# A graph layer on one core: how the node features x come into SBUF and are transposed

## The chip, the cores and the metric

The kernel runs on one core of a Trainium2 chip. What counts is the time of one execution on the device in microseconds (us). A core has five engines with instruction streams of their own: PE (matrix multiplications and transposes), DVE (elementwise work), ACT (elementwise work, copies), POOL (elementwise work, indirect DMAs) and SP (which here only issues DMAs). The transfers that SP, ACT and POOL issue share 16 DMA engines.

## The reference

Inputs are x (6250 nodes by 128 values, float32), and 100,000 edges, src and dst, sorted by dst. For each edge a small network works on the features of its two ends, the results are averaged over the edges that end in a node, and a second network and a layer norm follow:

```python
msg_in = concatenate([x[src], x[dst]], axis=-1)
h = relu(msg_in @ Wm1 + bm1)
h = relu(h @ Wm2 + bm2)
messages = h @ Wm3 + bm3
agg = segment_sum(messages, dst) / clip(count, 1)
upd = relu(concatenate([x, agg]) @ Wn1 + bn1) @ Wn2 + bn2
out = layernorm(x + (x + upd))
```

## The kernel before, in words

The first layer is split: x[src] @ (upper half of Wm1) and x[dst] @ (lower half) are worked out once per node, not once per edge. So there are three stages.

**Preparation**, up to about 85 us. x is loaded into `x_sb` (L172 to L180): tile t holds rows 128 t to 128 t + 127, one row on each partition, so a DMA of n tiles puts n separate rows of 512 bytes on each partition. The DMAs take 2, 2, 4, 8, 8, 8, 8 and 8 tiles, and one more takes the last 106 rows. Four tiles make a block, and there are 13 blocks (12 full ones and the rest). `turn` (L256 to L263) transposes a block's tiles on PE into one bank `pt` (L261), and ACT copies the bank to `xT` (L263), which holds x with nodes along the free axis. `a_table` (L234) multiplies two tiles of `xT` with one half of Wm1 (`products`, L230), ACT copies the products to a buffer of the pool `brow` (L239), and SP writes them to the table `atab` in HBM (L240). `b_table` (L242) does the same with the other half of Wm1 and splits the products into three bf16 terms, with ACT (L247), DVE (L248, L253) and POOL or ACT (L250, L252), before SP writes them to `btab` (L254). `brow` has six buffers, which both tables share; a buffer is free again when its write has landed. `x_part` (L304 to L315) works out x's part of the second network and puts it over `xT` and `x_sb`, whose first contents have then been used.

Beside that, `dst` and `src` are loaded (`load_rows`, L129) through ACT's and POOL's queues, DVE works out the window of nodes of each group of edges (L188 to L214, L268), and `starts` and `columns` (L272 to L302) spread it over the partitions. `dpad`, a copy of dst in HBM, is written by SP (L533).

The order of PE's instructions is written by hand (the loop at L329 to L344): transposes of block i + 1, then the products of block i for atab, then those of block i - 3 for btab. Up to the end of this stage the other engines' orders, SP's queue among them, come from a planner, which places instructions by estimated costs when the program is built. Each engine carries out its instructions in the order given, and waits on semaphores for what others produce.

**The edge loop**, to about 1131 us: 196 groups of up to 512 edges. POOL gathers rows of atab (L406), SP loads a window of btab (L412), and PE does the layers (L443, L449, L463) and the sums over nodes (L472, L483).

**The node stage**, to the end: blocks of 512 nodes, with a load of the nodes' reciprocal counts `rc` spread over all partitions (L662), the second network and the layer norm.

Of the kernel before, what the change touches and what calls it, by code (L numbers as in the profile page):

```python
# [19 lines left out]
P = 128  # L20
EPS = 1e-5
NONE = 16384
WN = 32
# [4 lines left out]
def kernel(  # L28
# [36 lines left out]
    nc = tc.nc  # L65
    N, D = x.shape
# [3 lines left out]
    GT = 4  # L70
# [4 lines left out]
    LT = -(-LAST // P)  # L75
    NT = -(-N // P)
    NTF = N // P
# [2 lines left out]
    R = NG // 2  # L80
    assert D == P and HC == 2 and NG == NGF + 1 and NG == 2 * R and R <= P
    assert E % 16 == 0 and (N - 1) + N // 16 * WB + WB < NONE
    assert LT == 2 and N < NONE and GT * WN == P

    assert N - 1 + WB + 1 <= NPAD and 3 * WB + 1 == NQ

# [10 lines left out]
    x_sb = const.tile([P, NT, D], F32, name="x_sb")  # L97
    xT = const.tile([P, NT * P], F32, name="xT")
# [30 lines left out]
    def load_rows(eng, t, edges):  # L129

        row = 2 * GE
        full = E // row // 16 * 16
        eng.dma_start(t[:full, :], edges[: full * row].rearrange("(r e) -> r e", e=row))
        for r in range(full, R):
            n = min(row, E - r * row)
            eng.dma_start(t[r:r + 1, :n], edges[r * row:r * row + n].rearrange("(r e) -> r e", r=1))
# [14 lines left out]
    with tc.tile_pool(name="prep", bufs=1) as prep, tc.tile_pool(  # L151
# [9 lines left out]
        with tc.high_priority():  # L161
            nc.scalar.dma_start(w1, wm1.rearrange("(k p) h -> p k h", p=P))
            load_rows(nc.scalar, dst_i, dst)
            load_rows(nc.gpsimd, src_i, src)
            with nc.allow_non_contiguous_dma(reason="a bias, one value a partition"):
                nc.gpsimd.dma_start(b1, bm1.rearrange("(c p) -> p c", p=P))
                nc.gpsimd.dma_start(b2, bm2.rearrange("(c p) -> p c", p=P))
                nc.gpsimd.dma_start(b3, bm3.rearrange("(c p) -> p c", p=P))
                nc.gpsimd.dma_start(bu1, bn1.rearrange("(c p) -> p c", p=P))
            nc.gpsimd.dma_start(nb2[:, 0, :], bm2.rearrange("(o h) -> o h", o=1).to_broadcast([P, H]))  # L170
            t = 0
            for n in (2, 2, 4, 8, 8, 8, 8, 8):  # L172
                n = min(n, NTF - t)
                nc.sync.dma_start(
                    x_sb[:, t:t + n, :],
                    x[t * P:(t + n) * P, :].rearrange("(t p) d -> p t d", p=P),
                )
                t += n
            assert t == NTF
            nc.sync.dma_start(x_sb[:N - NTF * P, NTF, :], x[NTF * P:, :])  # L180
# [75 lines left out]
        def turn(t0):  # L256
            m = min(4, NT - t0)
            pt = pp.tile([P, 4, P], F32, name="pt", tag="pp")
            for i in range(m):
                n = min(P, N - (t0 + i) * P)  # L260
                nc.tensor.transpose(pt[:, i, :n], x_sb[:n, t0 + i, :], ident[:n, :n])  # L261
            w = min(m * P, N - t0 * P)
            nc.scalar.copy(xT[:, t0 * P:t0 * P + w], pt.rearrange("p i n -> p (i n)")[:, :w])  # L263

# [60 lines left out]
        assert sorted(X_BESIDE + X_BEHIND + X_FIRST + X_END) == list(range(BLOCKS))  # L327

        turn(0)  # L329
        for i in range(BLOCKS + BEHIND):  # L330
            if i + 1 < BLOCKS:
                turn(4 * i + 4)
            if i < BLOCKS:
                for t0 in range(4 * i, min(4 * i + 4, NT), 2):
                    a_table(t0)
            if i == INDICES:
                starts()
            if i - INDICES in (1, 2):
                columns(i - INDICES - 1)
            if i >= BEHIND:  # L340
                for t0 in range(4 * (i - BEHIND), min(4 * (i - BEHIND) + 4, NT), 2):
                    b_table(t0)
            if BLOCKS - 1 <= i < BLOCKS - 1 + len(X_BESIDE):
                whole(x_part(X_BESIDE[i - BLOCKS + 1], bank_pb, (nc.scalar, nc.scalar)))  # L344
# [44 lines left out]
    with edge, tc.tile_pool(name="wk", bufs=2) as wk, tc.tile_pool(  # L389
# [136 lines left out]
        for i in range(NG + ahead + 1):  # L526
# [48 lines left out]
            m = g - 1  # L575
# [183 lines left out]
```

## Time and profile before

| what | value |
|---|---|
| median of 3 runs | 1212.57 us (1211.47 to 1213.6) |
| the profiled execution's own time | 1212.32 us |
| its span in the profile | 1210.5 us |
| PE busy | 1180.8 us (98%) |
| DVE, ACT, POOL busy | 669.9, 449.5, 805.9 us |
| first issue of x on SP, end of the last one | 0.77 us, 15.34 us |
| first write to atab issued | 18.79 us |
| first load from btab issued | 83.26 us |

How to read the profile. Times count from the start of the span. In lists of groups a line has: source line, engine, operation, what is written and read, partitions x elements and type, count, then busy us and the mean ns of one, then idle time ahead of them and what ended it. PEld is PE's weight load, which runs beside its multiplications. In the timeline a line has start, length, engine, source line, operation, count, and in brackets the idle time before it and what ended that. A busy PE is not PE at its peak, since the ends of its instructions are modelled. The DMA share is the mean busy share of the 16 DMA engines; it goes over 1 where packets overlap. Queue q1 is SP's, q10 ACT's and q0 POOL's.

### The profile page before, as it was taken

To read this page: it belongs to the slowest core of one execution; us is meant where nothing else is said; L and a number is where in the kernel's file an instruction comes from. 1 tells how busy PE (TensorE), PEld (TensorE's weight loads), DVE (VectorE), ACT (ScalarE), POOL (GpSimd) and SP (SyncE) were. 2 spreads that over 40 slices of the span, in tenths; PEclk is the share of its full clock that TensorE was granted. 3 is DMA by queue.
4 is the path that set the end of the run, shared out by engine and by line. 5 is a ranking of instruction groups with operands and counts; after the bars stand their busy time and mean duration, and the time that the engine had idled before them with its cause. 6 is when DMAs were issued, how large, how long until landed. Compare 5 with 4: busy or idle time off the path is not lost. (4 is left out here: it accounts for less than half of the span.)

```text
span 1210.5 us, 32797 instructions
## 1 busy us (share of the span) xinstructions
PE 1180.8 (98%) x11196; PEld 896.3 (74%) x11197; DVE 669.9 (55%) x2080; ACT 449.5 (37%) x1163; POOL 805.9 (67%) x859
## 2 busy tenths in 40 slices
PE   6989999999999999999999999999999999999996
PEld 5747777777777777777777777777777777777565
DVE  5764555545555555555555555555555555555586
ACT  4563333333333333333333333333333333333256
POOL 8267777777777777777777777777777777773220
PEclk9999999999999999999999999999999999999998
DMA  9886766666555555555555555555555555552333
GB/s 270 289 268 162 190 188 182 190 188 175 151 147 151 154 153 152 149 155 149 147 151 153 153 152 151 152 152 146 152 153 152 153 151 150 147 148 60 99 108 105
DMA packets 178152, 193.66 MB, mean 160 GB/s; under 512 B 30844, under 2 KB 151374, under 8 KB 177968
## 3 DMA queue, kind: packets, MB, share of 16 engines
q0 software_dynamic: 37984, 103.35, 31.0%
q1 hardware_dynamic: 111436, 61.93, 18.0%
q10 hardware_dynamic: 28564, 26.27, 7.9%
q8 instruction: 90, 1.47, 0.5%
q14 instruction: 78, 0.64, 0.2%
HBM read 168.92 MB, written 22.88 MB: 158 GB/s over the span
## 5 line engine op out<-in xcount | busy, mean ns | idle before, releaser
L406 POOL DMA_INDIRECT ag<-atab,srcT x784 | 753.2, 961 | 283.4 <-issue 184.3
L463 PE MATMUL ph<-w,h 128*128 128x256 f32 x3128 | 727.5, 386 | 0.9 <-ACT x_sb L312 0.9
L463 PEld LDWEIGHTS ph<-w,h 128*128 128x128 f32 x3128 | 578.3, 190 | 151.9 <-DVE acc L488 67.8
L454 ACT ACTIVATE h<-ph,b 128x256 f32<-128x256 f32 x782 | 306.3, 475 | 677.1 <-PE ph L449 500.7
L465 DVE TENSOR_TENSOR h<-ph,nb 128x512 f32<-128x512 f32 x391 | 270.4, 692 | 413.7 <-PE ph L463 411.2
L488 DVE TENSOR_TENSOR acc<-acc,pt 128x63 f32 x782 | 172.0, 220 | 33.4 <-PE ph L449 2.4
L443 PE MATMUL ph<-ident,ag 64*128 64x64 f32 x3128 | 130.3, 223 | 0.6 <-DVE b L376 0.6
L472 PE MATMUL pg<-h,oh 128*32 128x257 f32 x1564 | 125.6, 392 | 0.0
L443 PEld LDWEIGHTS ph<-ident,ag 64*128 64x128 f32 x3128 | 113.5, 139 | 2.8 <-ACT x_sb L312 1.5
L427 DVE TENSOR_SCALAR oht<-db,pbase 128x128 bf16<-128x128 int32 x392 | 105.1, 343 | 1.2 <-PE ph L449 0.7
L483 PEld LDWEIGHTS pt<-ident,part 64*128 64x128 f32 x1173 | 50.9, 136 | 66.8 <-issue 66.4
L449 PE MATMUL ph<-oht,bw 64*128 64x128 bf16 x1564 | 76.9, 217 | 2.4 <-DMA bw<-btab 2.0
L483 PE MATMUL pt<-ident,part 64*128 64x64 f32 x1173 | 77.8, 238 | 1.0 <-DVE acc L488 1.0
L475 ACT COPY part<-pg 128x257 f32<-128x257 f32 x196 | 76.7, 391 | 4.0 <-PE pg L472 4.0
L430 DVE TENSOR_TENSOR oh<-iota_n,dloc 128x128 f32<-128x128 f32 x196 | 55.1, 281 | 21.8 <-PE pg L472 21.1
L670 POOL TENSOR_TENSOR agg<-total,rc 128x512 f32<-128x512 f32 (+2 forms) x15 | 16.0, 1069 | 69.8 <-DVE total L667 62.7
L449 PEld LDWEIGHTS <-bw 64*128 64x128 bf16 x1564 | 53.7, 96 | 3.0 <-DMA bw<-btab 2.3
L230 PE MATMUL pbt<-w,xT 128*128 128x256 f32 x196 | 48.4, 392 | 3.7 <-ACT bt L239 3.0
L472 PEld LDWEIGHTS pg<-h,oh 128*32 128x32 f32 x1564 | 30.8, 108 | 21.7 <-issue 0.8
L230 PEld LDWEIGHTS pbt<-w,xT 128*128 128x128 f32 x196 | 36.5, 195 | 12.5 <-ACT bt L239 4.7
L250 POOL CAST bt<-rest 128x512 bf16<-128x512 f32 x18 | 12.8, 717 | 28.0 <-DVE rest L248 18.9
L692 PEld LDWEIGHTS pot<-wu,u 128*128 128x128 f32 (+1 forms) x196 | 24.0, 191 | 5.5 <-issue 4.8
(108 smaller groups left out, 415.1 us busy)
## 6 DMA issues: line engine op xcount, KB each, us to landing
bw<-btab SPq DMA_DIRECT2D x782, 32.0 KB
db<-in_dst_dram ACTq DMA_DIRECT2D x194, 128.0 KB
ag<-atab,srcT POOLq DMA_INDIRECT x784
btab<-bt SPq DMA_DIRECT2D x24, 384.0 KB
atab<-bt SPq DMA_DIRECT2D x24, 256.0 KB
xd<-in_x_dram SPq DMA_DIRECT2D x12, 256.0 KB
x2tab<-xd SPq DMA_DIRECT2D x12, 256.0 KB
x_sb<-in_x_dram SPq DMA_DIRECT2D x5, 512.0 KB
```

Source lines behind the costliest of these rows:

```text
L230: nc.tensor.matmul(pbt[:, a, :], xT[:, (t0 + a) * P:(t0 + a + 1) * P], w1[:, k, :], start=True, stop=True)
L406: nc.gpsimd.indirect_dma_start(out=ag[:, j, :], out_offset=None, in_=atab[:, :], in_offset=bass.IndirectOffsetOnAxis(ap=idx[:, j:j + 1], a ...
L427: nc.vector.tensor_scalar(oht[:n, k, :], db[:n, k * P:(k + 1) * P], pb_cols[:n, k:k + 1], None, op0=ALU.is_equal)
L443: nc.tensor.matmul(phs[h][:, c, u * NQ:(u + 1) * NQ], ag[halves[h], u, c * P:(c + 1) * P], ident[halves[h], halves[h]], is_transpose=True, ...
L449: nc.tensor.matmul(phs[h][:, c, k * P:(k + 1) * P], bw[halves[h], k, c * P:(c + 1) * P], oht[halves[h], k, :], start=False, stop=True, ski ...
L454: nc.scalar.activation(h1[:, c, h * 2 * P:(h + 1) * 2 * P], phs[h][:, c, :], AF.Relu, bias=b1[:, c:c + 1])
L463: nc.tensor.matmul(ph2[:, a, :], h1[:, c, (j0 + a) * P:(j0 + a + 1) * P], w2[:, c, :], start=(c == 0), stop=(c == HC - 1))
L465: nc.vector.tensor_tensor(h2[:, j0:j0 + 2, :H], ph2, nb2.to_broadcast([P, 2, H]), op=ALU.max)
L472: nc.tensor.matmul(pg[j * WN:(j + 1) * WN, :], oh[:, j, :], h2[:, j, :], start=True, stop=True, skip_group_check=True)
L475: nc.scalar.copy(part[:n, :], pg[:n, :])
L483: nc.tensor.matmul(pt[:, c, :], rows, ident[halves[h], halves[h]], is_transpose=True, start=True, stop=True, skip_group_check=True)
L488: nc.vector.tensor_add(window, window, pts[j // 2][:, :, k:k + WB])
```

## The change

x is laid out differently on the partitions. In a full block of four tiles, 512 rows, partition p now gets rows 4 p to 4 p + 3, which lie one after another in HBM: 2048 bytes in one piece. Tile i of the block then holds rows i, i + 4, i + 8 and so on. Block 0 comes in two DMAs of two tiles (1024 bytes on each partition), and DMAs of 4, 8, 8, 8, 8 and 8 tiles follow. The last tile stays as it was. PE's transposes are the same instructions, but the four quarters of `pt` now hold every fourth node. ACT's copy puts them back into the nodes' order: it reads `pt` along and writes `xT` with a step of four floats (16 bytes), 128 elements of quarter i and then those of quarter i + 1. What reads `xT` afterwards finds it as before.

```diff
-            t = 0
-            for n in (2, 2, 4, 8, 8, 8, 8, 8):
+
+            xb = x[:NTF * P, :].rearrange("(b p i) d -> p b i d", p=P, i=4)
+            for i0 in (0, 2):
+                nc.sync.dma_start(x_sb[:, i0:i0 + 2, :], xb[:, 0, i0:i0 + 2])
+            t = 4
+            for n in (4, 8, 8, 8, 8, 8):
                 n = min(n, NTF - t)
-                nc.sync.dma_start(
-                    x_sb[:, t:t + n, :],
-                    x[t * P:(t + n) * P, :].rearrange("(t p) d -> p t d", p=P),
-                )
+                nc.sync.dma_start(x_sb[:, t:t + n, :].rearrange("p (b i) d -> p b i d", i=4),
+                                  xb[:, t // 4:(t + n) // 4])
                 t += n
             assert t == NTF
             nc.sync.dma_start(x_sb[:N - NTF * P, NTF, :], x[NTF * P:, :])
...
             w = min(m * P, N - t0 * P)
-            nc.scalar.copy(xT[:, t0 * P:t0 * P + w], pt.rearrange("p i n -> p (i n)")[:, :w])
+            block = xT[:, t0 * P:t0 * P + w]
+            if m == 4:
+                nc.scalar.copy(block.rearrange("p (n i) -> p i n", i=4), pt)
+            else:
+                nc.scalar.copy(block, pt[:, 0, :w])
```

More of the change, by code (lines that the diff above doesn't have):

```diff
@@ L82 @@
     assert E % 16 == 0 and (N - 1) + N // 16 * WB + WB < NONE
-    assert LT == 2 and N < NONE and GT * WN == P
+    assert LT == 2 and N < NONE and GT * WN == P and NTF % 4 == 0 and NT == NTF + 1
     assert N - 1 + WB + 1 <= NPAD and 3 * WB + 1 == NQ
```

## The prediction

> **What bounds the kernel now.** I read the busy table in 10 us windows first, to see which stage the change can touch. Columns: window, its length, busy us (and instructions) of PE, PEld, DVE, ACT, POOL, then granted clock, mean busy share of the 16 DMA engines, GB/s.
>
> ```profile
> 0.00:10.00 10.00, 2.26 (x9) 1.51 (x11) 2.10 (x6) 1.89 (x3) 8.86 (x22) 1.00 0.85 208
> 10.00:20.00 10.00, 10.00 (x48) 8.59 (x48) 8.72 (x19) 5.56 (x10) 10.00 (x15) 1.00 1.18 275
> 20.00:30.00 10.00, 7.87 (x40) 6.30 (x39) 5.38 (x7) 5.66 (x10) 6.21 (x9) 1.00 0.94 330
> 30.00:40.00 10.00, 9.61 (x47) 7.88 (x46) 7.81 (x15) 5.86 (x11) 2.43 (x5) 1.00 0.78 279
> ```
>
> PE works almost without a gap from 10 us on, except in the third window. The page gives it 1180.8 of 1210.5 us. From about 85 us to 1131 us the edge loop is PE's alone and nothing in it changes. What is to be won lies where PE stands still in the preparation: 7.7 us of the first 10, and 2.1 us between 20 and 30. From 24.8 to 84 us PE is busy 56.66 of 59.2 us. The timeline of PE shows both places, and ACT's timeline what the second one waits for (start, length, instruction, idle before).
>
> ```profile
> 3.85 0.66 PE L261 MATMUL pt<-ident,x_sb 128*128 128x128 f32 x2 [3.85 <-DMA x_sb<-in_x_dram]
> 6.94 0.69 PE L261 MATMUL pt<-ident,x_sb 128*128 128x128 f32 x2 [2.44 <-DMA x_sb<-in_x_dram]
> 9.08 1.12 PE L261 MATMUL pt<-ident,x_sb 128*128 128x128 f32 x4 [1.45 <-DMA x_sb<-in_x_dram]
> 9.99 3.17 PE L230 MATMUL pbt<-w,xT 128*128 128x256 f32 x8
> 13.00 0.60 PE L261 MATMUL pt<-ident,x_sb 128*128 128x128 f32 x4
> 13.43 1.89 PE L230 MATMUL pbt<-w,xT 128*128 128x256 f32 x8
> 24.73 0.48 PE L230 MATMUL pbt<-w,xT 128*128 128x256 f32 x1 [2.04 <-ACT bt L239]
> ...
> 24.09 1.28 ACT L239 COPY bt<-pbt 128x512 f32<-128x512 f32 x2 [1.65 <-DMA atab<-bt]
> ```
>
> First place: PE's order has the transposes of block 1 ahead of the first products, and block 1 lands at 9.08. Second place: all six `brow` buffers hold rows of atab whose writes have not landed, so ACT's seventh copy waits until 24.09 and PE until 24.73. Both are DMA. The queue view then shows why (queue: packets, MB, share of 16 engines), for 5 to 7 us, for 13 to 18 us, and for 1142 to 1145 us, where rc is loaded (L662, 512 floats on each partition).
>
> ```profile
> q0 software_dynamic: 99, 0.38, 78.2%
> q1 hardware_dynamic: 111, 0.05, 13.7%
> ...
> q1 hardware_dynamic: 2862, 1.45, 120.9%
> ...
> q1 hardware_dynamic: 575, 1.04, 101.5%
> ```
>
> q1 is SP's queue. From 5 to 7 us x gets 0.05 MB while src_i (q0) gets 0.38 MB: packets of 512 bytes beside packets of 4096. From 13 to 18 us x is alone, the engines are full, and 512-byte packets move 290 GB/s. In the third stretch the engines are just as full, and 508 of the 575 packets are of 2 KB: 350 GB/s. That is the nearest row to what x will be.
>
> **What the Trainium skill says.** "DMA: Bandwidth & Descriptors", section "Queues, rings and completion order": a DMA engine takes turns between queues by packet. The 5 to 7 us stretch agrees (0.05 against 0.38 MB). Its section "Why small descriptors are slow (HBM only)" names a fixed cost in every packet; here 290 against 350 GB/s. "SBUF — State Buffer", section "Specifications (TRN2)": a cacheline is 16 bytes, two hits in a line are wanted for full bandwidth, and each new line costs. No ACT row of the kernel before steps through SBUF like that; DVE has one that agrees, below.
>
> **The change, part by part.** The profiled execution took 1212.32 us (span 1210.5 and 1.8 around it), 0.25 below the median of the runs, 1212.57. I subtract from 1212.3.
>
> 1. *Pieces of x.* Now 48 x 128 = 6144 of 512 bytes and 106 for the last tile. Then 256 of 1024 bytes (block 0, two DMAs), 11 x 128 = 1408 of 2048, and the same 106. SP issues eight DMAs and one, as before; today these hold SP until 15.3 us [...] (8 in 12.84 us, the first two in 0.45 us each), then at about 0.45 us each until 5 us. Behind them on SP stand w2, w3, wu1, dpad and the first atab write (18.79 now). SP being free earlier wins nothing alone: the writes stay behind x in the same queue.
>
> 2. *The DMA path to the first landing of atab.* By 8 us 0.47 MB of q1 has moved, so 2.7 MB of x are left, and they take until about 18.7. At 350 GB/s they take 2.7/0.350 = 7.7 us, plus some 0.5 us for the 0.15 MB of other queues: 8 + 8.2 = 16.2, so 2.5 us saved. Before 8 us the engines moved 275 GB/s for all queues; x there in larger pieces may give 0.2 more. Sum 2.7. Bounds: only the difference of the two clean rates, 3.145 MB x (1/0.293 - 1/0.350) = 1.75 us (2862 x 512 bytes in 5 us is 293); at the 377 GB/s of the stretch from 24 to 26 us, 2.7/0.377 = 7.2, so 3.2 us. The landing goes from 24.09 to 21.4.
>
> 3. *PE's own path to the same point.* With pieces of 2048 bytes x takes a larger turn beside src_i and dst_i. Block 1 (0.52 MB of x) lands at 9.08; between 0, if x stays starved, and 4 us, if x moved first at 250 GB/s (2.7 + 2.1). I take 1.5. ACT is free for its seventh copy at 22.44 now (end of L263's copy), so at 20.9 then, and without any stall it would be 1.5 + 2.04 = 3.5 us ahead.
>
> 4. *The smaller of the two counts.* ACT's seventh copy waits for a landing at 21.4, not 24.09, so PE resumes at 22.0, not 24.73: 2.7 us. Part of the stall (0.5 us) stays; x starting sooner is hidden behind it. After that PE's work is the same and moves as a whole: its remaining idle time to 84 us is 2.5 us, in waits of at most 0.9, and I take none of it.
>
> 5. *ACT's copy with a step (L263).* 12 instructions, 591 ns each now. They will write one float, then jump 16 bytes. DVE's L298 does this with a step of 32 bytes (862 ns for 392 elements), its L277 writes runs of 16 bytes (554 ns).
>
> ```profile
> L263 ACT COPY xT<-pt 128x512 f32<-128x512 f32 x12 | 7.1, 591 | 7.2 <-PE pt L261 7.2
> ...
> L298 DVE CAST srcT<-ps 128x392 int32<-128x392 f32 x2 | 1.7, 862 | 0.0
> ...
> L277 DVE COPY base<-spread 128x392 f32<-128x392 f32 x2 | 1.1, 554 | 0.0
> ```
>
> That is 0.79 ns more per element, 0.40 us for 512: 0.99 us a copy, 4.8 us in all. Low end: nothing, 0.59. High end: ACT pays by the line. L239 takes 587 ns for 512 elements and 372 for 256, so 0.84 ns each over 0.16 fixed; four times 0.43 is 1.71, and 1.87 us. What covers it: in blocks 1 to 3 PE turns over in 2.17 us (13.00 to 15.16), and ACT has two copies of 0.58 beside this one, so up to 1.01 us it hides. From block 4 on a turn is about 3.9 us against four copies, 2.34, so up to 1.56 hides. At 0.99 it costs nothing, by a narrow margin. Queued behind it on ACT are the copies of L239 and L247, for which PE (five pbt banks), DVE and the table writes wait; the block itself is needed only after the products of the block before, 1.9 us later.
>
> 6. *dst_i.* If x takes more of the early turns, dst_i lands after 10.9. Its DVE chain ends at 22.16 and DVE then waits 3.9 us for L247; PE needs it at 34.3. A slip of 1 us costs nothing.
>
> Sum: 1212.3 - 2.7 = 1209.6.
>
> **Rivals.** (B) PE's own path decides: SP, free at 5 us, puts the first atab writes ahead of dpad (0.39 MB, some 2 us around 21 us), or 2 KB packets run at 377 GB/s, and no stall is left: 1.5 to 2.5 plus 2.04, so 4.0 us, 1208.3. For it: SP's order is a planner's; against: dpad needs nothing and was placed early. (C) Hidden anyway: x remains starved and the writes find another wait, such as the weights or dpad ahead of them, or the DMA doesn't keep 2048 bytes in one piece (atab's 1024 and rc's 2048 speak against that). Gain 0.8 us, 1211.5. (D) Slower: ACT becomes the bound of the preparation. At 1.87 us blocks 1 to 3 lose 3 x 0.86 and blocks 4 to 12 lose 9 x 0.31, together 5.4 us, less 2.7: 1215.0. It decides from a copy of 1.6 to 1.7 us on; DVE's factor of 1.56 speaks against it.
>
> **How the numbers follow.** A 0.50, between 1.75 and 3.5 us: 1208.8 to 1210.6. B 0.20, C 0.18, D 0.12. The range reaches from B with PE starting up to 2 us earlier still and some later waits gone (1206.9) to C with a little of ACT's cost (1212.6); it leaves out most of D. What a measurement can tell from no change is 0.2%, 2.4 us, so faster means under 1209.9: some 0.38 of A's 0.50 and all of B, 0.58. Within: the rest of A, C, 0.29. Slower: D and a bad order on SP, 0.13.
>
> **What will show it.** Right: x in some 1,800 packets and about 350 GB/s before 17 us; PE's block 1 at 7 to 8 us; L239's wait on atab ending near 21.4; L263 at about 1 us; the first bw load (83.26 now) near 80.5. Wrong: L263 above 1.6 us; a stall in the same place ending at 24; an ACT wait in blocks 1 to 3 that was not there; the first bw load not moved although PE is ahead at 25 us.

## The result, and the profile after

| | before | after |
|---|---|---|
| median of 22 runs each, in turn on one chip | 1211.79 us | 1210.1 us (1207.34 to 1213.13) |
| ratio, with its 95% interval | | 0.9986 (0.998 to 0.9993) |
| the profiled execution's own time | 1212.32 us | 1208.8 us |
| its span | 1210.5 us | 1207.0 us |

The change gains 1.7 us, with an interval from 0.8 to 2.4 us. The prediction said 2.7, from 1212.3 to 1209.6, in a range down to 1206.9 and up to 1212.6. In two groups of runs further down the kernel before took 1453.71 and 1452.1 us. The kernels profiled in those groups show PE waiting some 145 us or more ahead of one line of the edge loop; why is open, so of those kernels only the preparation is compared with the others, and a ratio only with the kernel before in its own group.

Up to the edge loop the order of the instructions on every engine and on SP is the same before and after; what moved is when each could start. Line numbers after the x loads are 2 to 6 higher: L261 is now L263, ACT's copy L263 is L267, L230 is L232, L239 is L241.

First the windows of the kernel after that differ (columns as in the prediction: length, PE, PEld, DVE, ACT, POOL, clock, DMA share, GB/s).

```profile
0.00:10.00 10.00, 2.78 (x10) 1.94 (x12) 2.10 (x6) 2.64 (x4) 8.86 (x22) 1.00 0.83 238
10.00:20.00 10.00, 10.00 (x45) 8.55 (x44) 9.60 (x19) 7.13 (x10) 10.00 (x15) 1.00 1.03 313
20.00:30.00 10.00, 9.17 (x47) 7.47 (x46) 5.27 (x8) 6.44 (x10) 6.60 (x10) 1.00 0.81 285
```

Between 20 and 30 us PE is busy 9.17 us where it was 7.87: the hole has shrunk by 1.3. From 10 to 20 us it is as full as before, but with 45 instructions in place of 48: PE does less in the same time. The timeline of PE in the kernel after shows both.

```profile
3.45 0.66 PE L263 MATMUL pt<-ident,x_sb 128*128 128x128 f32 x2 [3.45 <-DMA x_sb<-in_x_dram]
5.00 0.69 PE L263 MATMUL pt<-ident,x_sb 128*128 128x128 f32 x2 [0.89 <-DMA x_sb<-in_x_dram]
8.57 1.11 PE L263 MATMUL pt<-ident,x_sb 128*128 128x128 f32 x4 [2.87 <-DMA x_sb<-in_x_dram]
9.47 3.62 PE L232 MATMUL pbt<-w,xT 128*128 128x256 f32 x8
12.88 1.06 PE L263 MATMUL pt<-ident,x_sb 128*128 128x128 f32 x4
13.74 1.98 PE L232 MATMUL pbt<-w,xT 128*128 128x256 f32 x8
...
21.61 0.60 PE L263 MATMUL pt<-ident,x_sb 128*128 128x128 f32 x4
22.05 1.03 PE L232 MATMUL pbt<-w,xT 128*128 128x256 f32 x4
23.91 2.97 PE L232 MATMUL pbt<-w,xT 128*128 128x256 f32 x12 [0.83 <-ACT bt L241]
```

The two halves of block 0 come 0.4 and 1.9 us earlier than before, block 1 only 0.5. PE then stands still for 2.87 us ahead of block 1, not 1.45, and works slowly behind it, for longer than in before: the same eight products take 3.62 us (3.17 before, 1.89 later on), the transposes of block 2 1.06 (0.60 before). The transposes of block 5, the last ones ahead of the old stall, start at 21.61; before, they started at 21.22. The stall is 0.83 us in place of 2.04, and PE goes on at 23.91 in place of 24.73. ACT's timeline shows what is left of it.

```profile
22.25 1.18 ACT L267 COPY xT<-pt 128x512 f32<-128x512 f32 x1 [2.74 <-PE pt L263]
23.17 1.17 ACT L241 COPY bt<-pbt 128x512 f32<-128x512 f32 x2
```

The seventh copy for atab (23.17) shows no wait for a landing any more. It stands in ACT's order behind block 5's copy with a step, which waits for PE's transposes and then takes over a microsecond. The landing is only just ahead of it, though. No view prints it, but the trace's semaphore records give it: the first write to atab has landed at 24.01 us in before (ACT goes on at 24.09) and at 23.05 here; 21.4 was forecast. All twelve of the copies with a step take 1110 ns, where 591 was the time before and 990 the prediction:

```profile
L267 ACT COPY xT<-pt 128x512 f32<-128x512 f32 x12 | 13.3, 1110 | 6.1 <-PE pt L263 6.1
```

The queue view of the kernel after, from 5 to 7 us and then from 13 to 16 us (queue: packets, MB, share of 16 engines; first line of the second: all queues together):

```profile
q0 software_dynamic: 83, 0.33, 63.1%
q1 hardware_dynamic: 80, 0.16, 34.1%
...
DMA packets 606, 1.13 MB, mean 375 GB/s; under 512 B 39, under 2 KB 73, under 8 KB 606
```

x gets 0.16 MB beside src_i from 5 to 7 us, where it got 0.05, so packets of 2048 bytes do take a larger turn; src_i still takes two thirds. Alone, x moves at 375 GB/s where it moved 290. SP's waits in the kernel after, up to 20 us (total us, times, longest), show what SP did with pieces that are quicker to issue:

```profile
SPq L183 <- DMA x_sb<-in_x_dram: 1.8, 1, 1.8
SPq L182 <- DMA x_sb<-in_x_dram: 1.7, 1, 1.7
SPq L178 <- DMA x_sb<-in_x_dram: 1.5, 2, 1.3
SPq L178 <- DMA dst_i<-in_dst_dram: 1.1, 1, 1.1
```

In the built program the DMAs of SP and ACT use eight completion semaphores in turn, and each waits until the one that had its semaphore has landed. So SP does not run free from 5 us on: x's issues end at 8.85 with the tail, w2 goes at 10.65, and the first write to atab at 17.06 (18.79 before).

### The profile page after: what moved, and what is told of

It reads as the page before. It is cut to its first block, busy times and chain, and to the rows that moved or that the text cites. A ratio compares the mean times of both kernels' runs of the same rounds, so it can differ in the third digit from the quotient of the medians.

```text
span 1207.0 us, 32797 instructions
## 1 busy us (share of the span) xinstructions
PE 1178.5 (98%) x11196; PEld 895.0 (74%) x11197; DVE 670.4 (56%) x2080; ACT 454.5 (38%) x1163; POOL 804.9 (67%) x859
## 5 line engine op out<-in xcount | busy, mean ns | idle before, releaser
L232 PE MATMUL pbt<-w,xT 128*128 128x256 f32 x196 | 48.7, 394 | 2.5 <-ACT bt L241 1.6
L232 PEld LDWEIGHTS pbt<-w,xT 128*128 128x128 f32 x196 | 36.8, 197 | 10.9 <-ACT bt L241 2.8
```

The source lines that it names most:

```text
L232: nc.tensor.matmul(pbt[:, a, :], xT[:, (t0 + a) * P:(t0 + a + 1) * P], w1[:, k, :], start=True, stop=True)
```

## Experiments

My theory after the result was: 2 KB pieces do move the landing as forecast, and three things take part of it back: PE's slow pace after the longer idle stretch, ACT's slow copy ahead of the seventh one, and a hold-up on the DMA engines that the rates show (below). The runs bear out the copy and the hold-up, and they do not bear out that the idle stretch sets the pace. Rivals: the step in ACT's write is free, and the landing explains all; or the landing does nothing, and what gain there is comes from block 1.

The positions on PE's timeline, in us. "Resumes" is the first product behind the old stall, with its wait; "x part" is the first product of `x_part` that PE waited for, at 64.35 before. A profile is one execution, and two of the same kernel differ by 0.3 at 24 us and 0.6 at 63 us (the two rows of after), so single rows are no measure of a gain below that. "Landed" is the landing of the first write to atab, from the semaphore records.

| kernel | block 1 | block 2 | block 5 | landed | resumes (wait) | x part | ratio to before (95%) |
|---|---|---|---|---|---|---|---|
| before | 9.08 | 13.00 | 21.22 | 24.01 | 24.73 (2.04) | 64.35 | 1 |
| after | 8.57 | 12.88 | 21.61 | 23.05 | 23.91 (0.83) | 63.47 | 0.9986 (0.998 to 0.9993) |
| after, again | 8.64 | 12.97 | 21.36 | 22.37 | 23.59 (0.76) | 62.84 | 0.9986 (0.9979 to 0.9992) |
| pieces alone | 8.47 | 12.80 | 21.24 | 21.52 | 23.00 (0.30) | 61.40 | 0.9972 (0.9961 to 0.9983) |
| step alone | 9.32 | 13.64 | 22.72 | 23.74 | 24.91 (0.72) | 63.96 | 1.0003 (0.9994 to 1.0012) |
| after, nb2 late | 8.36 | 12.48 | 20.70 | 20.98 | 22.92 (0.75) | 61.28 | 0.9976 (0.9967 to 0.9985) |
| before, nb2 late | 9.05 | 13.12 | 21.35 | 23.96 | 24.68 (1.87) | 64.09 | 0.9997 (0.9986 to 1.0008) |
| nb2 late, step in read | 8.81 | 13.13 | 22.24 | 21.21 | 24.00 (0.30) | 62.18 | 0.9972 (0.9961 to 0.9982) |
| PE kept busy | 8.76 | 11.77 | 19.99 | 21.39 | 22.22 (0.76) | 61.06 | 0.9976 (0.9967 to 0.9984) |

**The two halves of the change.** First the loads of after with ACT's old copy:

```diff
-            block = xT[:, t0 * P:t0 * P + w]
-            if m == 4:
-                nc.scalar.copy(block.rearrange("p (n i) -> p i n", i=4), pt)
-            else:
-                nc.scalar.copy(block, pt[:, 0, :w])
+            nc.scalar.copy(xT[:, t0 * P:t0 * P + w], pt.rearrange("p i n -> p (i n)")[:, :w])
```

> The 2048-byte pieces alone: x is loaded as after the change, ACT copies along as before, so the rows of xT, and with them of both tables, stand in another order than the nodes (that part of the computation is changed). Theory 1 (the loss is on the DMA side: the engines stood almost still from 11.5 to 14 us, and ACT's step costs little): 0.3 to 0.6 us faster than the changed kernel, so 1.9 to 2.4 below the kernel before, a first landing of atab still near 23.2 us, PE resuming at about 23.8. Rival (ACT's step, 1.11 us a copy instead of 0.59, took the gain): about 1 us or more faster than the changed kernel, near the 2.7 us forecast.

Measured: 1209.73 beside 1212.23 us, 2.5 apart in the medians; the ratio, 0.9972, is a gain of 3.4 us (2.1 to 4.7). Both are above the 1.7 of the whole change, with intervals that overlap a little. ACT, then PE, at the old stall in this kernel:

```profile
21.88 0.58 ACT L265 COPY xT<-pt 128x512 f32<-128x512 f32 x1 [3.25 <-PE pt L263]
22.36 1.08 ACT L241 COPY bt<-pbt 128x512 f32<-128x512 f32 x2
```

```profile
23.00 2.86 PE L232 MATMUL pbt<-w,xT 128*128 128x256 f32 x12 [0.30 <-ACT bt L241]
```

The seventh copy starts 0.48 us after block 5's copy, where in the kernel after it starts 0.92 after it, and PE waits 0.30 us, not 0.83. A measure that PE's pace does not enter is the time from block 5 on PE to its resuming. It is 1.76 us here and in all five kernels below whose ACT writes along and which keep this order, and 2.19 to 2.30 in the five profiles in which it writes with a step. So the step costs some 0.45 us at this place. In the first profile of after two things hold the seventh copy at once: without the step the landing at 23.05 would have held it until about 23.13 (in before it starts 0.08 behind the landing), and it starts at 23.17. In the second profile, with the landing at 22.37, it is the step alone.

Then ACT's copy with a step, on the loads of before:

```diff
-            xb = x[:NTF * P, :].rearrange("(b p i) d -> p b i d", p=P, i=4)
-            for i0 in (0, 2):
-                nc.sync.dma_start(x_sb[:, i0:i0 + 2, :], xb[:, 0, i0:i0 + 2])
-            t = 4
-            for n in (4, 8, 8, 8, 8, 8):
+            t = 0
+            for n in (2, 2, 4, 8, 8, 8, 8, 8):
```

> ACT's step alone: x is loaded in 512-byte pieces as before, the copy to xT writes with a step of 16 bytes, so the rows of xT stand in another order than the nodes (that part of the computation is changed). Theory 1: a copy takes 1.11 us, the kernel is 0 to 0.6 us slower than before, since PE waits for atab's landing at 24.1 us in any case. Rival: 1 to 2 us slower.

ACT's copies with the step, PE at block 1, and ACT's seventh copy:

```profile
L265 ACT COPY xT<-pt 128x512 f32<-128x512 f32 x12 | 13.4, 1115 | 6.5 <-PE pt L261 6.5
...
9.32 1.11 PE L261 MATMUL pt<-ident,x_sb 128*128 128x128 f32 x4 [1.56 <-DMA x_sb<-in_x_dram]
...
24.22 1.12 ACT L239 COPY bt<-pbt 128x512 f32<-128x512 f32 x2
```

Measured: 1212.14 us, ratio 1.0003, so the step costs nothing that can be measured on the loads of before. Its copies are just as long, 1115 ns. The table shows the cover: PE reaches block 5 at 22.72, 1.5 us later than in before (0.24 of it with block 1, the rest by its pace, since it waits for nothing in between), and yet it resumes only 0.18 later. In this profile the slow copy lets the seventh one go at 24.22, 1.50 behind block 5. With block 5 at 21.22 as in before, that would be 22.7, 1.3 us ahead of the landing: the late landing then hides the step, and the loads of the change take that cover away. The two halves, +0.4 and -3.4 us by the ratios, add to -3.0 where the whole is -1.7 (by the medians -0.1 and -2.5): the sign is what this cover would give, though each of the numbers is known only to about 1 us.

**The hold-up on the DMA engines.** From 11 to 14 us, still in the middle of x, the engines of the kernel after move less than those of before. Before, then after:

```profile
11.00:14.00 3.00, 3.00 (x14) 2.49 (x13) 2.97 (x3) 1.39 (x3) 3.00 (x4) 1.00 1.20 277
```

```profile
11.00:14.00 3.00, 3.00 (x10) 2.44 (x10) 2.96 (x5) 1.19 (x3) 3.00 (x4) 1.00 0.89 210
```

In that stretch POOL's queue carries nb2, a row spread over all partitions (128 KB). I moved that load behind the weights in SP's queue, once in the kernel after and once in that of before:

```diff
-            nc.gpsimd.dma_start(nb2[:, 0, :], bm2.rearrange("(o h) -> o h", o=1).to_broadcast([P, H]))
...
         nc.sync.dma_start(wu1, wn1.rearrange("(k p) h -> p k h", p=P))
+        nc.sync.dma_start(nb2[:, 0, :], bm2.rearrange("(o h) -> o h", o=1).to_broadcast([P, H]))
```

> The changed kernel with the load of nb2 (one row of 1 KB spread over 128 partitions) taken from POOL's queue, where it runs beside x at 11 to 14 us, and put on SP behind wu1. Theory 1 (packets of nb2 hold single DMA engines up to 2.4 us and all others wait): the stretch from 11 to 14 us moves over 330 GB/s, the first landing of atab comes about 1.5 us sooner (21.6), the kernel is about 1 us faster than the changed one. Rival (the engines stood still for another reason, such as SP's waits for earlier DMAs): landing within 0.4 us of 23.2, time within 0.5 us of the changed kernel.

> The same move of nb2 in the kernel before, as the control for it. Theory 1: with 512-byte pieces the packets of nb2 took 0.3 us and nothing stood still, so the move gains 0.2 to 0.5 us (its 0.13 MB leaves that stretch but stays ahead of atab). Rival: it gains as much as in the changed kernel, and then it says nothing on the change.

The same window in the kernel after with nb2 late:

```profile
11.00:14.00 3.00, 3.00 (x15) 2.53 (x14) 3.00 (x4) 1.91 (x3) 3.00 (x5) 1.00 1.03 385
```

With nb2 on POOL's queue the same window has 210 GB/s in after, 289 in after's second profile, 248 with the pieces alone and 268 to 275 in three kernels below; without it 385 here and 323 to 393 in the four others with nb2 late. So nb2 there does hold x up, by an amount that varies. It reaches the landing: 20.49 to 21.21 us in the five kernels with the new loads and nb2 late, 21.30 to 23.05 in the six profiles with the new loads and nb2 on POOL's queue. With the loads of before, nb2 late changes nothing there (23.96 for 24.01). The times: 1209.23 us in the kernel after, 0.9976, a gain of 2.9 us where the change alone gives 1.7; the intervals overlap. In the kernel of before, 0.9997: nothing that can be measured. In both, ACT's order differs too from about 30 us on (a cast for btab goes ahead of a copy to xT), so the edit moves more than nb2. How the lost rate would get to PE is not shown, though. From 9 to 21 us PE waits for no part of x in the kernel after, at the old stall it waits behind the slow copy and not for the landing, and of the 0.91 us that this kernel is ahead at block 5, 0.21 is block 1's landing and the rest PE's pace (the products behind block 1 take 3.38 and block 2's transposes 0.60). So the rate and the landing are shown, and their worth to the time is not.

**Where the step costs nothing.** The same order of nodes can be had with the step on another side: ACT reads `pt` with a step and writes `xT` along, or PE's transposes write `pt` with a step and ACT copies straight.

```diff
-                nc.scalar.copy(block.rearrange("p (n i) -> p i n", i=4), pt)
+                nc.scalar.copy(block.rearrange("p (n i) -> p n i", i=4), pt.rearrange("p i n -> p n i"))
```

> The changed kernel with the step on the other side of ACT's copy: it writes xT along and reads the bank pt with a step of 512 bytes. Theory 1 (ACT pays for writes that each meet a new 16-byte line of SBUF): a copy takes 0.6 to 0.7 us, PE resumes 0.4 to 0.5 us sooner, the kernel is 0.3 to 1.5 us faster than the changed one, as with the pieces alone. Rival (the jump costs the same on either side): 1.0 to 1.2 us a copy and the time of the changed kernel.

```diff
-                nc.tensor.transpose(pt[:, i, :n], x_sb[:n, t0 + i, :], ident[:n, :n])
+                to = pt.rearrange("p i n -> p (i n)").rearrange("p (n i) -> p n i", i=4)[:, :, i] if m == 4 else pt[:, i, :n]
+                nc.tensor.transpose(to, x_sb[:n, t0 + i, :], ident[:n, :n])
...
+            nc.scalar.copy(xT[:, t0 * P:t0 * P + w], pt.rearrange("p i n -> p (i n)")[:, :w])
```

> The changed kernel with the nodes' order made by PE: each transpose writes its column of the bank pt with a step of four floats, and ACT copies along. Theory 1: a copy is back at 0.59 us; a transpose costs what it did (four in 0.60 us) or up to twice that, 12 x 0.6 us at most, most of it on the bound engine. With free transposes the time is that of the pieces alone, some 3 us below the kernel before; with doubled ones 5 us are lost and it is slower than the changed kernel. Rival (the step's 0.52 us on ACT costs nothing): no faster than the changed kernel even if the transposes are free.

ACT's copies with the step in the read, and then, in the other kernel, PE's transposes and ACT's copies:

```profile
L267 ACT COPY xT<-pt 128x512 f32<-128x512 f32 x12 | 7.1, 590 | 8.4 <-PE pt L263 8.4
```

```profile
L264 PE MATMUL pt<-ident,x_sb 128*128 128x128 f32 x48 | 8.7, 305 | 8.8 <-DMA x_sb<-in_x_dram 8.8
...
L266 ACT COPY xT<-pt 128x512 f32<-128x512 f32 x12 | 7.1, 591 | 9.5 <-PE pt L264 9.5
```

The copy is back at 590 and 591 ns, and a warm group of four transposes takes 0.60 us as before. At the old stall PE waits 0.30 us in both. The ratios to a kernel before of 1453.71 us were 0.999 (0.9977 to 1.0002) and 0.9983 (0.9976 to 0.9991), which say little about the 1212 us kernel. In the second one block 1 landed at 10.15 us in its profile, and PE resumed at 24.64 in spite of the short wait. The step seems to cost something behind the stall too: from resuming to the x part, with nb2 on POOL's queue, the three profiles with a short copy (pieces alone and these two) take 38.40 to 38.77 us, the three with the step (after twice, PE kept busy) 38.84 to 39.56, on average 0.6 more.

With nb2 late as well, ACT's step in the read was run beside a kernel before of 1212.21 us:

> The changed kernel with nb2 late and ACT's step on the reading side, where a copy took 590 ns. Theory 1: both hold-ups are gone, so PE resumes at 22.9 us with 0.3 us of wait, the first load from btab goes out at 79.6, and the kernel is 3 to 4.5 us below the kernel before and 1.5 to 2.5 below the changed one. Rival (nb2 and the step are one gain): 2.9 us below the kernel before, as with nb2 late alone.

1208.75 us, ratio 0.9972, a gain of 3.5 us (2.2 to 4.7). That overlaps a little with the interval of after, and nearly in full with that of nb2 late alone (0.9967 to 0.9985), so the rival, one gain and not two, is not excluded. Its wait at the old stall is 0.30 as it should be. But its profile has PE resuming at 24.00, later than after, since PE came to block 5 at 22.24: its slow pace, of which the next part tells. PE's step with nb2 late ran in the group of 1453.71 us:

> The changed kernel with nb2 late and the nodes' order made by PE's transposes. Theory 1: both gains, 1.2 us for nb2 and up to 1.5 for the step, add up in part, 3.5 to 4.5 us below the kernel before, if a transpose costs the same. Rival: the two are one gain (either takes away the same wait of PE near 23 us), so 2.9 to 3.4 us as with each alone.

Ratio 0.9944 (0.9926 to 0.9963); block 5 at 21.18, PE resumes at 22.94 with 0.30 of wait. The saved ACT time shows in the wait. The ratio has another base: it is a gain of some 8 us of 1453.71, above the 3.5 to 4.5 forecast, and why is open.

**PE's pace.** Ten spare transposes of the identity between those of block 0 and of block 1, into a `pt` bank that nobody reads, fill the idle stretch before block 1:

```diff
         turn(0)
+        spare = pp.tile([P, 4, P], F32, name="spare", tag="pp")
+        for i in range(10):
+            nc.tensor.transpose(spare[:, i % 4, :], ident, ident)
```

> The changed kernel with ten transposes of the identity on PE between the transposes of block 0 and of block 1, into a spare bank that nothing reads, about 2.9 us of work while PE waits for block 1. Theory 1 (PE runs its first 20 instructions after an idle stretch at half its pace, 0.45 instead of 0.24 us, and the longer idle stretch ahead of block 1 gave back what the earlier landing had won): the eight products of block 0 take 1.9 to 3.0 instead of 3.62 us, the transposes of block 2 start 0.6 to 1.7 us sooner, and the kernel is 0.3 to 1.5 us faster than the changed one. Rival (the pace belongs to a fixed time after the start, or the products wait for data): the products take 3.2 us or more as before, and the time is that of the changed kernel.

> The changed kernel once more, so that the three beside it have it on their own chip. It is expected 1.7 us below the kernel before (0.9 to 2.4), a copy to xT of 1.11 us, no wait of ACT for the landing of atab near 23 us, PE resuming at 23.9.

PE's timeline of the kernel with spare transposes:

```profile
6.55 2.34 PE L338 MATMUL spare<-ident 128*128 128x128 f32 x10
8.76 1.12 PE L263 MATMUL pt<-ident,x_sb 128*128 128x128 f32 x4
9.67 2.27 PE L232 MATMUL pbt<-w,xT 128*128 128x256 f32 x8
11.77 0.60 PE L263 MATMUL pt<-ident,x_sb 128*128 128x128 f32 x4
...
22.22 3.01 PE L232 MATMUL pbt<-w,xT 128*128 128x256 f32 x12 [0.76 <-ACT bt L241]
```

Block 1 landed no earlier (8.76), but the products behind it take 2.27 us, not 3.62, and block 2's transposes 0.60. PE is 1.2 us ahead of the second run of after at block 2 (11.77 against 12.97), 1.4 ahead when it resumes, and 1.8 at the x part; the time is 1209.01 us, ratio 0.9976, beside 1210.61 and 0.9986 for after in the same group. More work on PE made the kernel faster, by 1.2 us by the ratios and 1.6 by the medians, though the two intervals overlap a little (0.9967 to 0.9984, and 0.9979 to 0.9992).

The Trainium skill, "TensorE: Matmul & The Clock Gate", Part 1 on the HAM clock gate, says that PE's array runs at half clock by default and after an idle window of about 3.4 us, that it comes to full clock after about as long a busy one, and that these windows run freely, so that the moment differs from run to run. The trace agrees: eight products take 3.62 us at first and 1.89 later, and the trace's clock records begin, at full clock, at 12.56 us in before, 13.90 in after, 13.31 in its second profile and 10.41 with the spare transposes. Ahead of its first record the column of the granted clock counts 1.00, so it doesn't show this.

So PE is slow at the start, and work ahead of block 1 ends that sooner. That the longer idle stretch makes it last longer, as the expectation has it, is not shown. From block 1 to block 5 PE takes 12.14 us in before, behind 1.45 us of idling, and 13.04 in after, behind 2.87. But it takes 13.40 behind 1.56 with the step alone, 13.18 behind 0.64 with src_i moved (below), and 12.39 behind 2.87 in PE's step with nb2 late:

```profile
8.79 1.11 PE L264 MATMUL pt<-ident,x_sb 128*128 128x128 f32 x4 [2.87 <-DMA x_sb<-in_x_dram]
9.70 3.42 PE L232 MATMUL pbt<-w,xT 128*128 128x256 f32 x8
12.95 0.60 PE L264 MATMUL pt<-ident,x_sb 128*128 128x128 f32 x4
```

In the twelve profiles without spare transposes the two do not go together at all (correlation -0.02). The first clock record comes 3.5 to 6.1 us behind block 1 in them; the three with the old loads take 12.14 to 13.40 us to block 5, the nine with the new ones 12.34 to 13.43. So how long PE stays slow differs from execution to execution (5.3 us behind block 1 in the first profile of after, 4.7 in the second), and whether the change lengthened it on average is open.

**Block 1 earlier.** src_i's load moved behind the biases on POOL's queue, on top of nb2 late:

```diff
-            load_rows(nc.gpsimd, src_i, src)
...
                 nc.gpsimd.dma_start(bu1, bn1.rearrange("(c p) -> p c", p=P))
+            load_rows(nc.gpsimd, src_i, src)
```

> The changed kernel with nb2 late, and src_i issued on POOL's queue behind the four biases, some 3 us later. Theory 1 (src_i's packets of 4096 bytes starve x at 5 to 8 us): block 1 lands at 6.5 to 7.3 instead of 8.4 us, PE's first blocks move 1 us forward, and the kernel is 0 to 1 us faster than with nb2 late alone, since the next wait (ACT's seventh copy, behind the copy of block 5) moves with PE. Rival (x waits for dst_i on ACT's queue or for its own issue): block 1 lands at 8 us or later as before.

PE's timeline, then ACT's seventh copy:

```profile
6.74 0.69 PE L263 MATMUL pt<-ident,x_sb 128*128 128x128 f32 x2 [2.91 <-DMA x_sb<-in_x_dram]
8.07 1.12 PE L263 MATMUL pt<-ident,x_sb 128*128 128x128 f32 x4 [0.64 <-DMA x_sb<-in_x_dram]
8.97 3.62 PE L232 MATMUL pbt<-w,xT 128*128 128x256 f32 x8
12.39 1.06 PE L263 MATMUL pt<-ident,x_sb 128*128 128x128 f32 x4
...
21.25 0.60 PE L263 MATMUL pt<-ident,x_sb 128*128 128x128 f32 x4
21.69 2.76 PE L232 MATMUL pbt<-w,xT 128*128 128x256 f32 x12
...
21.17 1.22 ACT L241 COPY bt<-pbt 128x512 f32<-128x512 f32 x2 [1.92 <-DMA atab<-bt]
```

The forecast did not come true. x got 0.40 MB from 5 to 7 us, not 0.16, but block 1 landed at 8.07, only 0.3 ahead of the 8.36 with nb2 late alone, and block 0's second half came later, at 6.74. SP waited 2.7 us for an earlier load of x before it issued the next. So src_i is not the only thing that holds block 1 up; what else does is open. In this kernel the planner put the seventh copy ahead of block 5's copy on ACT: it waits for the landing, at 21.17, and PE then goes through the place of the old stall without a wait there. So which of the two PE meets depends on the order on ACT. (Ratio 0.9959, 0.9945 to 0.9974, in the group of 1453.71 us.)

**All three.** nb2 late, the step in ACT's read, PE kept busy:

> The changed kernel with all three: nb2 late, ACT's step on the reading side, and ten spare transposes that keep PE busy ahead of block 1. Theory 1 (three separate hold-ups, each of 1 us or a little more at first): the transposes of block 2 start at 11.8 us, those of block 5 at 20.0, PE resumes at 21.5 to 22 with 0.3 us of wait, and the kernel is 4 to 5.5 us below the kernel before. Rival (something behind them, the first landing of atab or DVE's chain, takes over once they are gone): 3.4 us or less below, as with two of them, and PE waits near 22 us for a landing or for DVE.

```profile
11.28 0.60 PE L263 MATMUL pt<-ident,x_sb 128*128 128x128 f32 x4
...
19.50 0.60 PE L263 MATMUL pt<-ident,x_sb 128*128 128x128 f32 x4
...
21.26 3.11 PE L232 MATMUL pbt<-w,xT 128*128 128x256 f32 x12 [0.30 <-ACT bt L241]
```

PE resumes at 21.26, 2.65 us ahead of after and 3.5 ahead of before, and comes to the x part at 59.47: the best of all. Its landing wait has not come back even there, with the landing at 20.49 and the seventh copy at 20.62. Its time was taken beside a kernel before of 1452.1 us, 1442.14, ratio 0.9935 (0.9921 to 0.9949), some 9.5 us, about twice what was forecast. What it gives beside 1212 us was not measured.

## Why the prediction was right, and where it was not

1. *Pieces of x (step 1).* Right in the pieces, wrong for SP, which was to be free at about 5 us. It waits for earlier loads to land and issues the tail at 8.54.

2. *The landing (step 2, 2.7 us).* Mis-sized. It moved by 0.96 us in the first profile (24.01 to 23.05) and by 1.64 in the second (22.37), not by 2.7. The rate of x alone, 375 GB/s, is above the 350 that I took. What the sum left out is nb2 on POOL's queue, beside which all queues together fell to 210 to 289 GB/s; with nb2 late the landing comes at 20.49 to 21.21, as early as I forecast or earlier. In after no instruction is seen to wait for it; in the first profile it came just 0.1 us too early for that.

3. *PE's own path (step 3, 1.5 us earlier).* **This is the step that failed.** Block 1 came 0.5 us earlier (8.57 for 9.08), not 1.5: src_i still took two thirds of the engines' bytes from 5 to 7 us, and moving src_i brought only 0.3 us more. And I took block 1's landing for a shift of everything behind it, but PE was 0.39 us *later* at block 5, and 0.14 later in the second profile. From the starts in the two timelines: -0.51 to block 1, +0.39 from there to block 2 (4.31 for 3.92), +0.51 from there to block 5 (8.73 for 8.22), in all +0.39. What I left out is that PE works at about half its pace at first, for 3.5 to 6.1 us behind block 1, at an end that block 1 doesn't set. In before the landing hid this: the step alone was 1.5 us later at block 5 and 0.18 at resuming. In after nothing hides it. How much of the 0.39 is the change's and how much the single execution's is not shown.

4. *The smaller of the two counts (step 4).* The rule held, its outcome was turned round. I had the landing decide with 0.5 us of stall left; PE's and ACT's path decides, and 0.83 us of wait is left with another cause. And the stall was never worth its 2.04 us: 0.30 of wait stays in the kernels with a short copy, so without the landing PE would have resumed at 21.22 + 1.76 = 22.98, 1.75 earlier. The account of the measured gain at the old stall: the wait falls by 1.21 us (2.04 to 0.83), 0.39 of that is eaten by the later block 5, and PE is 0.82 ahead (24.73 to 23.91). That PE's work then moves as a whole is right as far as the x part, where it is 0.88 ahead; in the second profile of after it is 1.14 and 1.51 ahead. The first load from btab, forecast near 80.5, goes out at 83.05 and 81.56 (83.26 before), so in the first profile little of it gets that far. The medians say 1.7, and I have not placed the rest. The profiled spans differ by more, 3.5 us: with a granted clock of 0.50 PE ran for 6.83 us from 87.66 and 3.41 us from 1135.55 in the profile of before, and for 3.41 us from 89.00 in that of after.

5. *ACT's step (step 5).* The size was off by a little, 1.11 us for 0.99, and the cover by more. I set the copy against the mean time of a turn, with 1.56 us of room from block 4 on. But at block 5 what counts is the order: PE may go on with only four products (1.03 us) after the transposes, and the bank for the next is freed by the seventh copy, behind the slow one. Beside that one place the cover was right in the blocks that I named: in the kernel after PE has no wait on ACT in blocks 1 to 3, which the forecast named as the sign of trouble. At the old stall it costs some 0.45 us, and perhaps 0.6 more behind it. Over the whole kernel the pieces alone gained more than the full change, by 1.7 us in the ratios and 0.8 in the medians, with intervals that overlap; with nb2 late, the step in the read instead of the write was worth 0.5 in both.

6. *dst_i (step 6).* Nothing in the profiles speaks against it: PE's wait on that chain, ahead of L303, is 0.72 us in after and was 0.51.

Of the rivals, B had the right place (PE's path decides, the landing is no longer waited for) with a gain by block 1 that did not come. D, ACT as the bound, is excluded by 1.11 us, but its mechanism, an ACT copy that PE waits behind, is there at one block. The gain, 1.7, lies just below A's 1.75 to 3.5. It came from A's landing, which was no longer waited for, less two costs that I had put at nothing, the slow copy and PE's pace. That the time fell within the range does not bear out the working: block 1 brought a third of what I took and the landing about half, and the range was wide enough to hold both errors.

## What to carry to other kernels

When a wait is removed, work out what the next one in line is from the order of instructions at that very place; a mean over a turn hides a copy that stands ahead of the one that frees a bank. A cost that hides behind a stall is free only as long as the stall is there: try each half of a change alone, as here the step was free on its own and made PE wait some 0.45 us longer in company. A wait that is no longer seen may be only just gone: look for when the thing it waited for now comes, here 23.05 us for a copy at 23.17. And an earlier first piece of work isn't an earlier finish while the engine is still slow: check the pace of equal instructions, in more than one profile, before you give the difference a cause.

## What the runs showed of the hardware

- ACT writing SBUF with a step of 16 bytes takes 1110 ns for 128x512 float32, 591 without: 1.01 ns more per element. The Trainium skill, "SBUF — State Buffer", Specifications (TRN2), says that each access on a new 16-byte line pays, which agrees. No run varied the step, so that it is the line that costs, and not the step as such, is not shown here.
- ACT reading PSUM with a step (590 ns) and PE's transposes writing PSUM with a step of 16 bytes (0.60 us for four) cost nothing that shows. "PSUM — Partial Sum Buffer", Specifications (TRN2), says that any access pattern that isn't contiguous slows matmuls significantly. For these float32 transposes the measurement says otherwise, and it decides.
- Packets of 2048 bytes from HBM move 375 GB/s where packets of 512 moved 290, both alone. Beside a load that spreads one row over the partitions on POOL's queue all queues together fell to 210 to 289 in six profiles, and without that load there they moved 323 to 393 in five. With the packets of before it made no difference (277 and 276 with it, 270 without). Why the engines stand idle there is not shown.
- PE works at about half its pace until 3.5 to 6.1 us of nearly unbroken work behind block 1, however long it idled before (0.64 to 3.21 us); ten spare transposes ahead of block 1 ended that at 10.41 us instead of 13.31 and 13.90.
